# A gather on TensorE with its 128 output channels written as two instructions of 64 each

## The chip, the cores and the metric

The kernel runs on one core of one Trainium2 chip. The metric is the device time of one execution in microseconds (us). The kernel before took 786.88 us, the median of 3 runs (786.35 to 787.31). The profile shows one further execution; it took 786.77 us, of which the instructions' span covers 784.9 us.

## What is computed

All data is fp32. Layer 0 makes, for each pixel of 4 images of 256 channels and 64 x 64 pixels, 49 softmax weights and sums 49 shifted copies of the input with them. Layer 1 is a bottleneck block with batch statistics. Cut to what matters:

```python
# layer 0, x is (4, 256, 64, 64)
k = conv(x, w1, 7x7, dilation 2, padding 6) + b1      # 128 channels
attn = softmax(conv(k, w2, 1x1) + b2, axis=1)         # 49 weights per pixel
shifts = stack([xp[:, :, 2*u:2*u+64, 2*v:2*v+64] for u in range(7) for v in range(7)])
y = einsum('bkchw,bkhw->bchw', shifts, attn)
# layer 1
h = relu(bn(conv(y, w1, 1x1)))     # 256 -> 64 channels
h = relu(bn(conv(h, w2, 3x3)))     # 64 -> 64
return relu(bn(conv(h, w3, 1x1)) + y)   # 64 -> 256
```

## The kernel before

**Up to 490 us** the kernel computes the 49 weights per pixel: strided rows of the input are transformed on VectorE (the helper `stt`, L149), multiplied on TensorE (`column_convs`, L260), and turned into a matrix of weights by transposes (`turn`, L577). The weights end in `amat`, a part of the tile `arena`: for each image, column and parity the matrix that maps input rows to output rows.

**From 490 to 643 us** the gather runs together with layer 1's first conv; this is the part that the change touches. A unit is one image and one of four row and column parities; there are 16 units (L142). For each unit two tiles of input pixels by channels are needed: `x`, which three transfers load from HBM (`load_xt`: L111 and L117 small ones of 32 or 96 partitions, L112 the main one of 896 KB), and `t`, which is `x` shifted by 64 partitions (`shift_xt`: ScalarE copies one half, L121, GpSimd the other, L122 and L123). `more_xt` does this for unit n + 2 once unit n has been gathered, into the same tiles (two pairs alternate).

`gather(n, half)` makes 128 of the 256 channels of a unit. It takes two banks of PSUM, one for each column parity c, and issues 8 matmuls for each: seven for the tiles i = 1 to 7 with c = 0, the same for c = 1, and then the two edges (i = 0). The stationary operand is 128 pixels by 128 channels of `x` or `t`; the moving one is 128 columns of `amat`, in pieces of four elements. So a gather is 16 matmuls, and the stage has 32 gathers. The c = 0 matmuls read `x`, the c = 1 matmuls read `t`. Each fp32 matmul appears in the profile as two records of weight load and two of matmul, so that L765 has 1024 of each.

`keep_y` copies the two banks to a tile of SBUF, four copies for a gather: VectorE for half 0 (L786), ScalarE for half 1 (L784). Then SyncE's queue writes the tile to HBM (L787). `bank(0)` deals the gather's banks from five in turn.

`conv1` makes 64 channels from 256, for two units at once: 8 matmuls of 512 moving columns, whose outputs go to the partitions 0 to 63 (a = 0) or 64 to 127 (a = 1) of one bank. Two instructions that follow each other go to different halves. VectorE takes the statistics (L806) and copies a half (L812), ScalarE copies the other (L814).

The loop over units is: gather half 0; for an even n from 2 on `conv1` of the two units before; keep half 0; gather and keep half 1; load for n + 2. This part has no order written out by hand: a scheduler with its own estimates of cost orders each engine's instructions, and the DMA issues of SyncE. On TensorE it keeps the order of the loop, but for one place: the conv1 that belongs to unit 10 is broken up, and parts of unit 10's gather stand between its matmuls.

**From 643 us** the rest of layer 1 follows: direct and transformed 3x3 convs (L965, L977), transposes (L1040) and 64-channel products for the last batch statistics (`moments`, L1045, 65 moving columns, outputs to the two halves of the partitions in turn), and the last conv with the residual (L1027, L1084).

Of the kernel before, what the change touches and what calls it, by code (L numbers as in the profile page):

```python
# [48 lines left out]
P = 128  # L49
# [5 lines left out]
NT = H // 8  # L55
# [8 lines left out]
NP = len(PAIRS)  # L64
PIECES = ((0, 16), (16, 24), (40, 24))
READY = ((0, 1), (1, 4), (4, NT))
ROWS2 = 16
NS, WS = 4, 8
KV = K7 * K
# [24 lines left out]
def conv_seq_kernel(ctx: ExitStack, tc: tile.TileContext, xp, xt, w1, b1, w2t, b2, m1t, g1, be1,  # L94
                    m2t, g2, be2, m3t, g3, be3, z, mask, pavg, out, ydram):
    nc = tc.nc
# [41 lines left out]
    amat = arena[:, :AT].rearrange("p (g x c m e) -> p g x c m e", g=2, x=R // 2, c=2, e=4)  # L138
# [12 lines left out]
    def zero_rows(t):  # L151

        for k, i0, i1 in ((0, 0, 2), (1, 0, 1), (0, NR - 1, NR), (1, NR - 2, NR)):
            nc.gpsimd.memset(t[:, k, :, i0:i1], 0.0)
# [3 lines left out]
    def sort_x(raw, b, r0, n, dst, w0, last=None, first=None):  # L158

        d = dst.rearrange("p k (w b e) i -> p k w b e i", b=B, e=Q)  # L160
        nw = d.shape[2]
        for k in range(2):
            m = r0 // 2 + (r0 // 2 + 3 + k) % 2
            count = ((r0 + n) // 2 - m + 1) // 2
            i = (m + 3) // 2
            for a in range(2):
                lo = 2 * m + a - r0
                (last if last and k + a == 2 else first if first and k + a == 0 else nc.scalar.copy)(  # L168
                    d[:, k, :, PLACE[b], 2 * a : 2 * a + 2, i : i + count],
                    raw[:, lo : lo + 4 * count - 3 : 4, PAD + 2 * w0 : PAD + 2 * w0 + 2 * nw].rearrange(  # L170
                        "p r (w c) -> p w c r", c=2
                    ),
                )
# [41 lines left out]
    def rows_of(t, cols=slice(None), tiles=(0, NT)):  # L215


        def row(n):
            i = n // 2 + 2 * tiles[0]
            return t[:, n % 2, cols, i : i + 2 * (tiles[1] - tiles[0]) - 1 : 2]  # L220

        return row
# [50 lines left out]
    with ExitStack() as s1:  # L273
# [13 lines left out]
        with ExitStack() as s2:  # L287
# [71 lines left out]
            def early(n, cols=slice(None), parts=(even, odd, mix)):  # L359

                p, _, left = passes[0]
                t0, t1 = READY[n]
                x0, x1 = (xi[:, i, cols, t0:t1] for i in range(2))
                row = rows_of(slots, cols, READY[n])
                if even in parts:
# [78 lines left out]
        def fill_stage(h):  # L444
            zero_rows(stage)
            for r0 in range(0, H, ROWS2):
                for b in range(B):
                    raw = rawp.tile([P, ROWS2, WP], F32, tag="raw", name="raw")
                    nc.sync.dma_start(out=raw, in_=xp[b, P:, r0 : r0 + ROWS2, :])
                    sort_x(raw, b, r0, ROWS2, stage, R // 2 * h)  # L450

# [56 lines left out]
    for g in range(2):  # L508
        half = slice(g * MID, (g + 1) * MID)
# [165 lines left out]
    o = 4 * XT  # L675
# [3 lines left out]
    o = OUTER - NH1  # L679
# [33 lines left out]
    o = NH1  # L713
# [3 lines left out]
    o = 7 * C * 4  # L717
# [29 lines left out]
    def bank(kind):  # L747

        n_bank[kind] += 1
        return accall[:, 5 * kind + n_bank[kind] % (5 - 2 * kind)]  # L750

    def gather(n, half):

        b, q = units[n]
        m = (b // 2 * Q + q) * 2 * NT
        pts = [bank(0) for c in range(2)]
        for edge in (False, True):
            for c in range(2):
                x = xts[b, q, c]
                for i in (0,) if edge else range(1, NT):  # L760

                    o = 64 * (i - 1)
                    blocks = slice(m, m + 2 * NT, 2 * NT - 1) if edge else slice(m + 2 * i - 1, m + 2 * i + 1)
                    dst = pts[c].rearrange("p (m n) -> p m n", n=64)
                    nc.tensor.matmul(  # L765
                        dst[:, :: NT - 1] if edge else pts[c][:, o : o + 128],
                        x[:, i, half * P : (half + 1) * P],
                        amat[:, b % 2, :, c, blocks, :].rearrange("p x m e -> p m x e"),
                        start=(i == 1),
                        stop=edge,  # L770
                        skip_group_check=True,
                    )
        return pts

    def keep_y(n, half, pts):
# [41 lines left out]
    for n in range(len(units)):  # L817
        pts = gather(n, 0)
        if n and n % 2 == 0:
            conv1(*units[n - 2])  # L820
        if n == 9:
            clear_h1(1)
            nc.gpsimd.memset(w2blk, 0.0)
            for k, (j, a, o_a) in enumerate(TAPS3):
                d = TAP_ROW3[k]
                nc.sync.dma_start(
                    out=w2blk[a * MID : (a + 1) * MID, 3 * j : 3 * j + 3, o_a * MID : (o_a + 1) * MID],
                    in_=m2t[:, 3 * d : 3 * d + 3, :],
                )
        keep_y(n, 0, pts)  # L830
        keep_y(n, 1, gather(n, 1))
        if n + 2 < len(units):
            more_xt(n + 2)
# [175 lines left out]
    o = 4 * 2048  # L1009
# [24 lines left out]
    blocks = [(slot, i, q) for slot in range(2) for i in range(2) for q in range(Q)]  # L1034
    for n, (slot, i, q) in enumerate(blocks):
# [7 lines left out]
        for j in range(4):  # L1043
            for g in range(2):
# [4 lines left out]
                    start=(n == 0 and j == 0),  # L1049
                    stop=(n == len(blocks) - 1 and j == 3),  # L1050
                    skip_group_check=True,
# [14 lines left out]
    for half in range(NH):  # L1066
        c = slice(half * P, (half + 1) * P)
# [8 lines left out]
    blocks = [(slot + 2 * g, i, half) for slot in range(2) for i in range(2) for half in range(NH) for g in range(2)]  # L1076
    for k, (b, i, half) in enumerate(blocks):
        o = ops[k % 4]

        n = 256 if k in (0, len(blocks) - 1) else 512  # L1080
        for lo in range(0, 512, n):
            for q in (0, 2, 1, 3):
# [5 lines left out]
                dst = o[:, rows].rearrange("p (r a) (w c) -> p a c r w", a=2, c=2)[:, q // 2, q % 2]  # L1088
# [60 lines left out]
```

## Time and profile before

| what | value |
|---|---|
| median of 3 runs | 786.88 us |
| profiled execution | 786.77 us, span 784.9 us |
| TensorE matmul busy | 724.4 us, 92% of the span |
| VectorE, ScalarE, GpSimd busy | 74%, 39%, 11% |
| L260, column products | 2000 records, 384.4 us |
| L765, gather | 1024 records, 118.1 us, all between 490.4 and 638.8 us |
| L798, conv1 | 128 records, between 508.5 and 642.3 us |
| TensorE's granted clock in the stage from 488 to 645 us | 1.00 |
| DMA share in that stage | 0.65, 213 GB/s |

A line of a group names the line of the code, the engine, the operation, the tiles it writes and reads, the shapes, the number of records and their summed and mean time. A matmul's recorded duration includes its way through the array, and records overlap; how fast they follow each other is read from their starts. PEld is the weight load, which has its own records beside PE. `SPq` are the DMA issues of SyncE.

### The profile page before, as it was taken

To read this page: it belongs to the slowest core of one execution; us is meant where nothing else is said; L and a number is where in the kernel's file an instruction comes from. 1 tells how busy PE (TensorE), PEld (TensorE's weight loads), DVE (VectorE), ACT (ScalarE), POOL (GpSimd) and SP (SyncE) were. 2 spreads that over 40 slices of the span, in tenths; PEclk is the share of its full clock that TensorE was granted. 3 is DMA by queue.
4 is the path that set the end of the run, shared out by engine and by line. 5 is a ranking of instruction groups with operands and counts; after the bars stand their busy time and mean duration, and the time that the engine had idled before them with its cause. 6 is when DMAs were issued, how large, how long until landed. Compare 5 with 4: busy or idle time off the path is not lost.

```text
span 784.9 us, 10969 instructions
## 1 busy us (share of the span) xinstructions
PE 724.4 (92%) x4208; PEld 581.8 (74%) x4208; DVE 578.9 (74%) x685; ACT 305.2 (39%) x601; POOL 89.6 (11%) x155
## 2 busy tenths in 40 slices
PE   1969998999999989989999999999999979987996
PEld 1959887887888878878888888988877763436642
DVE  5799899999699689999998867233332247574796
ACT  4617465005621012111111158434443346346497
POOL 3416100001000010000003013222212200000000
PEclk9979998999999999999999999999999998997997
DMA  8741389626996985111110013666776659352298
GB/s 348 326 164 42 132 298 363 230 95 223 301 369 239 347 294 169 42 42 29 54 42 1 3 58 103 212 218 215 230 242 215 215 205 385 107 170 73 108 394 356
DMA packets 59814, 150.27 MB, mean 191 GB/s; under 512 B 7410, under 2 KB 35698, under 8 KB 56178
## 3 DMA queue, kind: packets, MB, share of 16 engines
q1 hardware_dynamic: 51792, 141.12, 50.4%
q10 hardware_dynamic: 7970, 8.45, 3.1%
q8 instruction: 33, 0.54, 0.3%
q14 instruction: 19, 0.16, 0.1%
HBM read 93.81 MB, written 55.74 MB: 191 GB/s over the span
## 4 chain that ended last, share of the span: by engine, by line
PE 58%; DVE 23%; DMA 8%; ACT 5%; issue 5%; ACTq 1%; POOL 0%; SPq 0%; DVEq 0%; POOLq 0%
PE acc L260 30%; DVE arena L149 13%; PE acc L765 12%; DVE arena L1084 4%; PE acc L798 4%; PE pconv L977 4%; PE pdirect L965 3%; DMA outer<-in_xt_dram 2%; DMA raw<-in_xp_dram 2%; PE acc L577 2%; DMA aside_dram<-sv 2%; DVE stage_x L149 1%; ACT arena L168 1%; PE pturn L1040 1%; ACT arena L584 1%
## 5 line engine op out<-in xcount | busy, mean ns | idle before, releaser
L260 PE MATMUL acc<-arena 128*128 128x196 f32 (+3 forms) x2000 | 384.4, 355 | 14.3 <-DVE arena L346 6.4
L260 PEld LDWEIGHTS acc<-arena 128*128 128x128 f32 x2000 | 323.8, 193 | 73.9 <-issue 13.1
L149 DVE SCALAR_TENSOR_TENSOR arena<-arena 128x1024 f32<-128x1024 f32 (+6 forms) x192 | 293.3, 1568 | 23.3 <-PE acc L260 17.0
L765 PEld LDWEIGHTS acc<-arena,outer 128*128 128x128 f32 x1024 | 115.5, 192 | 13.0 <-issue 10.9
L765 PE MATMUL acc<-arena,outer 128*128 128x128 f32 x1024 | 118.1, 276 | 4.9 <-issue 3.8
L806 DVE BATCH_NORM_STATS2 st<-acc 128x6 f32<-128x512 f32 x16 | 11.2, 699 | 68.3 <-PE acc L798 68.1
L284 ACT COPY sv<-acc 128x392 f32<-128x392 f32 x40 | 19.1, 484 | 92.3 <-PE acc L260 73.4
L168 ACT COPY stage<-raw 128x128 f32<-128x128 f32 x128 | 43.9, 417 | 23.6 <-DMA raw<-in_xp_dram 22.4
L1027 PE MATMUL pconv<-arena,w3m 64*128 64x512 f32 (+1 forms) x144 | 43.4, 597 | 0.6 <-DVE arena L1084 0.6
L121 ACT COPY outer<-outer 64x2048 f32<-64x2048 f32 x15 | 28.4, 1895 | 39.1 <-DMA outer<-in_xt_dram 39.0
L149 DVE SCALAR_TENSOR_TENSOR outer<-outer 128x784 f32<-128x784 f32 (+2 forms) x47 | 36.8, 835 | 3.6 <-ACT outer L919 3.6
L618 ACT COPY acc<-bks 128x392 f32<-128x392 f32 x40 | 18.3, 488 | 53.8 <-DVE outer L603 28.6
L601 ACT COPY outer<-acc 128x784 f32<-128x784 f32 x8 | 6.5, 813 | 79.7 <-PE acc L260 79.7
L1027 PEld LDWEIGHTS pconv<-arena,w3m 64*128 64x128 f32 x144 | 21.2, 189 | 21.6 <-DVE arena L1084 15.7
L786 DVE COPY bks<-acc 128x256 f32<-128x256 f32 x32 | 11.3, 416 | 33.4 <-PE acc L765 33.4
L122 POOL COPY outer<-outer 64x1792 f32<-64x1792 f32 x15 | 25.1, 1675 | 92.7 <-DMA outer<-in_xt_dram 92.6
L1089 ACT ACTIVATE outer<-arena 128x512 f32<-128x512 f32 (+1 forms) x58 | 34.7, 695 | 1.3 <-DVE arena L862 1.1
L1084 DVE SCALAR_TENSOR_TENSOR arena<-pconv,arena 128x512 f32<-128x512 f32 (+1 forms) x58 | 34.3, 666 | 0.0
L584 ACT COPY arena<-acc 128x512 f32<-128x512 f32 x52 | 27.1, 716 | 14.8 <-PE acc L577 14.4
L977 PE MATMUL pconv<-outer,arena 128*128 128x512 f32 x72 | 31.1, 592 | 0.0
L168 POOL COPY arena<-raw 128x192 f32<-128x192 f32 (+2 forms) x24 | 25.3, 1085 | 40.2 <-DVE arena L149 24.4
L798 PE MATMUL acc<-outer,w1m 128*64 128x512 f32 x64 | 29.6, 600 | 0.0
(147 smaller groups left out, 664.3 us busy)
## 6 DMA issues: line engine op xcount, KB each, us to landing
raw<-in_xp_dram SPq DMA_DIRECT2D x36, 608.0 KB, 5.4
outer<-in_xt_dram SPq DMA_DIRECT2D x17, 896.0 KB, 6.3
out_dram<-outer SPq DMA_DIRECT2D x14, 1024.0 KB, 4.5
arena<-y_dram SPq DMA_DIRECT2D x25, 512.0 KB, 8.0
fsort_dram<-stage SPq DMA_DIRECT2D x2, 4864.0 KB, 14.6
arena<-fsort_dram SPq DMA_DIRECT2D x8, 1216.0 KB, 9.3
y_dram<-outer SPq DMA_DIRECT2D x16, 512.0 KB, 5.4
aside_dram<-sv ACTq DMA_DIRECT2D x40, 196.0 KB, 5.5
```

Source lines behind the costliest of these rows:

```text
L121: nc.scalar.copy(t[:MID], x[MID:])
L122: nc.gpsimd.tensor_copy(t[MID:, : NT - 1], x[:MID, 1:])
L149: nc.vector.scalar_tensor_tensor(out, in0, scalar, in1, ALU.mult, ALU.add)
L168: (last if last and k + a == 2 else first if first and k + a == 0 else nc.scalar.copy)(d[:, k, :, PLACE[b], 2 * a : 2 * a + 2, i : i + count],
L260: nc.tensor.matmul(acc[i][d][:, o : o + (hi - lo) * K], xi[:, i, CW * w : CW * w + CW, :].rearrange("p x t -> p (x t)"), u[i][:, lo * K : ...
L584: nc.scalar.copy(dst, src)
L765: nc.tensor.matmul(dst[:, :: NT - 1] if edge else pts[c][:, o : o + 128], x[:, i, half * P : (half + 1) * P], amat[:, b % 2, :, c, blocks, ...
L798: nc.tensor.matmul(pt[a * MID : (a + 1) * MID, :], w1m[:, n, :], ys[a, n][:, 512 * i : 512 * i + 512], start=(n == 0), stop=(n == NH - 1), ...
L977: nc.tensor.matmul(m[k], wu[:, k, j, :], vs[k][:, g, j : j + R, :], start=(j == 0), stop=(j == 1))
L1027: nc.tensor.matmul(pt[:, :n], w3m[part, half * P : (half + 1) * P], h2[part, slot, q, lo : lo + n], start=True, stop=True)
L1084: nc.vector.scalar_tensor_tensor(v, conv3(b, q, i, half, lo, n), sc3[:, half : half + 1], v, ALU.mult, ALU.add)
L1089: nc.scalar.activation(dst, v.rearrange("p (r w) -> p r w", w=R), AF.Relu, bias=sh3[:, half : half + 1])
```

## The change

Each matmul of the gather becomes two. The first has the channels 0 to 63 of the half as its stationary operand and writes the partitions 0 to 63 of the bank, the second has the channels 64 to 127 and writes the partitions 64 to 127. Both have the same moving operand of 128 columns. The two stand next to each other in the program.

```diff
+HALVES = (slice(0, 64), slice(64, 128))
...
-                    nc.tensor.matmul(
-                        dst[:, :: NT - 1] if edge else pts[c][:, o : o + 128],
-                        x[:, i, half * P : (half + 1) * P],
-                        amat[:, b % 2, :, c, blocks, :].rearrange("p x m e -> p m x e"),
-                        start=(i == 1),
-                        stop=edge,
-                        skip_group_check=True,
-                    )
+                    for part in HALVES:
+                        nc.tensor.matmul(
+                            dst[part, :: NT - 1] if edge else pts[c][part, o : o + 128],
+                            x[:, i, half * P + part.start : half * P + part.stop],
+                            amat[:, b % 2, :, c, blocks, :].rearrange("p x m e -> p m x e"),
+                            start=(i == 1),
+                            stop=edge,
+                            skip_group_check=True,
+                        )
```

Nothing else of the program's text is changed; two lines are added, so that lines from 67 on stand one further down in the changed kernel, and lines from the matmul on two.

## Prediction, on record before the changed kernel ran

> **What bounds the kernel now.** I began with the page: TensorE is busy for 92% of the span, and the chain that ended last has 11.7% of the time on L765 and 3.7% on L798. Then I took the groups by line for the durations, the timeline of TensorE from 508 us on for the order, and the timelines of ScalarE and of SyncE's queue for what the stops in it wait on. From the page:
>
> ```profile
> PE 724.4 (92%) x4208; PEld 581.8 (74%) x4208; DVE 578.9 (74%) x685; ACT 305.2 (39%) x601; POOL 89.6 (11%) x155
> L765 PEld LDWEIGHTS acc<-arena,outer 128*128 128x128 f32 x1024 | 115.5, 192 | 13.0 <-issue 10.9
> L765 PE MATMUL acc<-arena,outer 128*128 128x128 f32 x1024 | 118.1, 276 | 4.9 <-issue 3.8
> ```
>
> In the gather the weight loads are busy as long as the matmuls. The timeline of TensorE shows their pace:
>
> ```profile
> 507.81 0.72 PE L765 MATMUL acc<-arena,outer 128*128 128x128 f32 x5
> 508.46 0.64 PE L798 MATMUL acc<-outer,w1m 128*64 128x512 f32 x1
> 508.47 0.64 PE L798 MATMUL acc<-bks,w1m 128*64 128x512 f32 x1
> 508.94 0.59 PE L798 MATMUL acc<-outer,w1m 128*64 128x512 f32 x1
> ...
> 511.52 0.59 PE L798 MATMUL acc<-outer,w1m 128*64 128x512 f32 x1
> ...
> 512.05 12.55 PE L765 MATMUL acc<-arena,outer 128*128 128x128 f32 x110
> 524.82 2.25 PE L765 MATMUL acc<-arena,outer 128*128 128x128 f32 x18 [0.22 <-issue]
> ```
>
> Three readings. First, the pace: 110 records take 12.55 us; less the last one's 0.275 us and one late step of 0.213, that is 108 steps of **111.7 ns**. The matmul alone does not need that: L260's of 147, 196 and 245 columns start 125, 166 and 206 ns apart, 0.83 ns a column, so 109 at 128, and L577's transposes of 128 columns do start 109 apart. Where L260 has 49 columns, its weight loads still follow each other 112 ns apart. So the gather goes at the pace of its 128-column weight load, with the matmul 2.5 ns behind. Second, conv1's two halves run together: both start at 508.46, and pairs follow every 0.43 us. Third, each change between the gather (128*128) and conv1 (128*64) costs time.
>
> The stop at 524.82 is a chain of its own:
>
> ```profile
> 515.74 1.20 ACT L784 COPY outer<-acc 128x256 f32<-128x256 f32 x4 [1.20 <-issue]
> 522.82 1.90 ACT L121 COPY outer<-outer 64x2048 f32<-64x2048 f32 x1 [5.88 <-DMA outer<-in_xt_dram]
> ```
>
> ```profile
> 513.94 0.38 SPq L112 DMA_DIRECT2D outer<-in_xt_dram  x1
> 514.41 2.89 SPq L787 DMA_DIRECT2D y_dram<-outer  x2
> 517.39 0.47 SPq L111 DMA_DIRECT2D outer<-in_xt_dram  x1
> 517.95 0.52 SPq L117 DMA_DIRECT2D outer<-in_xt_dram  x1
> ...
> 572.54 0.33 SPq L787 DMA_DIRECT2D y_dram<-outer  x1
> 572.92 0.43 SPq L112 DMA_DIRECT2D outer<-in_xt_dram  x1
> ```
>
> Unit 2's second gather ends at 515.6; L784 copies it out, L787 writes it, and behind it in SyncE's queue L111 and L117 load unit 4's edges. L121 shifts them until 524.7, and the c = 1 half of unit 4's gather starts: 9.1 us after 515.6. It then takes 18 records, conv1 and 32 records to the end of unit 4's second gather. So a round of two units lasts 9.1 + 50 steps + conv1, and the 78 steps beside it (unit 3 and half of 4) leave a gap. Units 4, 6, 8, 12 and 14 wait so (0.38, 0.41, 0.33, 1.99, 1.63 us over the step); rounds of 18.5 us, the last two 20.1 and 19.8.
>
> **The change part by part.**
>
> *Pace of the gather.* 1024 records of 128 output channels become 1024 pairs of 64. That adds 1024 weight loads and 1024 matmuls. The nearest rows are L798 and L1045, whose halves also alternate:
>
> ```profile
> 719.84 0.69 PE L1045 MATMUL moments<-outer 128*64 128x65 f32 x16
> 720.46 0.33 PE L1040 MATMUL pturn<-ident,arena 128*128 128x128 f32 x1
> 720.72 1.15 PE L1045 MATMUL moments<-outer 128*64 128x65 f32 x32
> 721.80 1.42 PE L1040 MATMUL pturn<-ident,arena 128*128 128x128 f32 x11
> 723.15 0.69 PE L1045 MATMUL moments<-outer 128*64 128x65 f32 x16
> ```
>
> Single records of L1045 at 729.935, 729.994, 730.052 and on show a pair every 58.5 ns, with two weight loads of 64 columns in it: the loads of the halves overlap too, so they hold no pair of 128 columns up. Between 58.5 ns at 65 columns and 429 at 512, a line gives **110.7 ns** at 128. Below, 109 (the matmul alone); above, twice 58.5, 117, if short pairs are limited by something that grows with their number; and twice 109, 218, if the halves cannot run together on this operand, which is a rival. I take 110.7, as both neighbours are pairs: 1.0 ns less a step.
>
> *Changes of shape.* Into conv1: last record of L765 at 508.255 (507.81 + 0.72 - 0.275), next start 508.46, 0.205 instead of 0.112; the first pair then holds 0.48 instead of 0.43. That is 0.144 us. Out of it: 511.52 to 512.05 instead of 0.43, and the next step 0.213 instead of 0.112: 0.20 us. All 10 entries and 9 exits from 508 to 639 us are like that, 3.2 us in all. With both in 128*64 they should go; the new one, from L577's transposes at 490.4, costs 0.1 more than now. The least that may go is nothing, if a change of 128 to 512 columns is what costs; L260's steps between widths show no such price, so I take all.
>
> [...]
>
> *Orders that move.* The scheduler gives new orders, read by comparing the programs. conv1 at unit 10 is whole: 8 entries and 7 exits are left. SyncE's queue now has L112 for unit 10 ahead of the second L787, so at about 569.5 instead of 572.92, when the first store has gone; elsewhere L787 of half 0 goes ahead of L112, ready about 0.1 us around it. L111 and L117 stay behind the second L787. VectorE's two L812 stand behind the four L786; nothing waits for them soon. ScalarE's L121 for odd units goes ahead of both L814, which then end at 515.2 (512.16 + 1.90 + two of 0.58), still before L784 at 515.74: hidden by 0.5 us, and each 0.1 us beyond it would go on the chain. GpSimd's order is unchanged. No wait is added; the copies out of PSUM wait for both halves of a bank, which end 7 ns apart.
>
> *The sum*, stretch by stretch:
> - 490.4 to 508.5: 160 steps at 1.0 ns, 0.16, less the dearer entry, 0.1: nothing.
> - Five rounds of the chain: 0.34 for the changes and 50 steps at 1.0 ns, 0.39 each: -1.95. The steps off the chain only widen the gap.
> - Unit 10: from 578.3 to the start of its second gather at 588.18 the trace has 9.9 us for 32 steps (3.54) and conv1 (3.43), so 2.9 us of waiting and three entries and exits. With L112 3 us earlier, L117 still issued near 573.4 and L121 ahead of L784, some 0.4 us of waiting stays: -2.5 (between -1.0, the changes alone, and -2.8).
> - From 624.5 on: one exit, two entries, 96 steps: -0.6.
>
> Together -5.05 us. From the profiled execution's 786.77 us that gives **781.7 us**; the median stands 0.11 us above it, which changes nothing. What follows at 643 us starts earlier by the same. At 109 ns it would be 781.1; at 117 (rounds of 128 x 0.117 + 3.48 = 18.46 us, no gap) 785.7. If the stores that go earlier in SyncE's queue also halved the five gaps (4.7 us), 779.3.
>
> **The rivals.**
>
> *The loads swallow it.* If the five rounds keep their length, because L117's landing (4.9 us here, 6.5 for unit 12) is set by the traffic and not by its issue, and unit 10 gains only its changes, 0.0 + 1.0 + 0.6 is left: 785.2 us. For it: two rounds are 1.5 us longer with the same work. Against: 213 GB/s in the stage, 453 at the most from 588 to 606.
>
> *Supply of instructions: slower.* A pair needs four instructions in 110.7 ns. L1040 and L1045 show 60 matmuls with their loads every 3.31 us (719.84 to 723.15), 55.2 ns a matmul, just what is needed (55.4), for some 10 us and with pauses. Over their whole stage, 710.6 to 731.63, it is 65.7 ns a matmul; that may be VectorE's pace, and may be the supply's. A round is then 128 pairs and 3.48 us with no gap left. Place: every stretch of L765. At 59.4 ns a matmul (118.8 a pair) the loss equals the gain; at 62.6, between the two rows, it adds 2.1 at the start, 1.0 in each of three rounds, 0.3 in two, 0.8 at the end, and unit 10 gains only 0.7: **792.6 us**.
>
> [...]
>
> *The halves do not run together.* The change would not do what it says: L798 and L1045 read runs of 64 bytes or more, the gather's moving operand pieces of 16 bytes, now twice at a time. One stream keeps up at 111.7. If they take turns, a pair costs 218 ns: 1024 x 0.1065 = 109 us less the changes and gaps, about 886 us.
>
> **How the numbers follow.** The forecast has 0.60, the swallowed gain 0.13, the supply 0.15, the turns (with all shares of them) 0.12. Two executions differ by 0.1%, so 0.2%, 1.6 us, can be told from no change. Faster: the forecast and half of the swallowed gain (785.2 lies on the edge), 0.67; same 0.06; slower 0.27. Range: from 777.5, two thirds of the gaps and unit 10's wait gone, to 793, which holds the supply and leaves out the turns.
>
> **What would show it.** Pairs of L767 (the new line) every 110 to 111 ns, weight loads no longer as busy as matmuls; first L800 after L767 at the normal step, and no 0.2 us step behind conv1; gaps before c = 1 still there, and at unit 10 under 0.5 us. A pace above 119, steps above 0.2 us around conv1, or rounds that stay at 18.5 us would prove me wrong.

## The result and the profile after

The changed kernel takes 783.38 us, the median of 22 runs (778.61 to 788.02), beside 786.90 us for the kernel before on the same chip (22 runs, 781.84 to 789.42). The ratio is 0.9964, with a 95% interval from 0.9947 to 0.9982: faster by 0.36%, where 0.66% had been forecast. The profiled execution took 784.71 us with a span of 782.9 us.

The lines of the page that answer to those of before; the gather is now L767:

```profile
PE 716.9 (92%) x5232; PEld 579.5 (74%) x5232; DVE 578.8 (74%) x685; ACT 304.7 (39%) x601; POOL 90.0 (12%) x155
L767 PEld LDWEIGHTS acc<-arena,outer 128*64 128x64 f32 x2048 | 112.7, 137 | 12.0 <-issue 11.4
L767 PE MATMUL acc<-arena,outer 128*64 128x128 f32 x2048 | 114.9, 273 | 6.7 <-issue 5.7
```

Twice as many records keep TensorE busy for 3.2 us less (114.9 for 118.1). The timeline of TensorE from conv1 of unit 2 on (L800 is conv1 now) shows how:

```profile
510.25 2.19 PE L767 MATMUL acc<-arena,outer 128*64 128x128 f32 x36 [0.45 <-issue]
512.23 0.59 PE L800 MATMUL acc<-outer,w1m 128*64 128x512 f32 x1
512.27 0.59 PE L800 MATMUL acc<-bks,w1m 128*64 128x512 f32 x1
...
515.27 0.59 PE L800 MATMUL acc<-arena,w1m 128*64 128x512 f32 x1
515.66 12.21 PE L767 MATMUL acc<-arena,outer 128*64 128x128 f32 x220
529.50 1.75 PE L767 MATMUL acc<-arena,outer 128*64 128x128 f32 x28 [1.62 <-issue]
```

The 220 records are 110 pairs. 12.21 us less the last record's 0.27 is 11.94 for 109 pairs and the offset of 0.04 between the halves. So a pair takes 109.2 ns where a whole product took 111.7. The first L800 record comes at once behind L767 (steps of 0.073 in place of 0.205 us), L767 follows conv1 after 0.39 us in place of 0.52, and its second step is normal. But the wait ahead of c = 1 in unit 4 is still there, and it is longer: 1.62 us idle where it was 0.22.

That wait is again the chain through ScalarE's copy (L786), the second store (L789), the edge loads (L112, L118) and the shift (L122). First ScalarE, then SyncE's queue, in the kernel after:

```profile
519.22 1.20 ACT L786 COPY outer<-acc 128x256 f32<-128x256 f32 x4 [0.81 <-ACT outer L816]
527.50 1.90 ACT L122 COPY outer<-outer 64x2048 f32<-64x2048 f32 x1 [7.08 <-DMA outer<-in_xt_dram]
```

```profile
517.11 0.34 SPq L789 DMA_DIRECT2D y_dram<-outer  x1
517.55 0.39 SPq L113 DMA_DIRECT2D outer<-in_xt_dram  x1
520.45 0.33 SPq L789 DMA_DIRECT2D y_dram<-outer  x1
520.87 0.38 SPq L112 DMA_DIRECT2D outer<-in_xt_dram  x1
521.34 1.01 SPq L118 DMA_DIRECT2D outer<-in_xt_dram  x1
```

Unit 2's second gather ends (start of its last pair) at 519.05. L118 is issued 2.29 us later; before it was 2.34. What has grown is the transfer: from L118's issue to the start of the shift it takes 6.16 us (521.34 to 527.50), where L117 took 4.87 (517.95 to 522.82). The interval from the end of one gather to the c = 1 half two units on, which the prediction kept at 9.1 us, came out like this (starts of single records, us):

| unit | 4 | 6 | 8 | 10 | 12 | 14 |
|---|---|---|---|---|---|---|
| before | 9.21 | 9.23 | 9.15 | 10.99 | 10.81 | 10.45 |
| after | 10.45 | 10.51 | 9.02 | 11.74 | 8.62 | 8.88 |
| after, second profile | 11.05 | 9.55 | 8.62 | 11.51 | 9.50 | 9.05 |

Without a wait it is 8.82 us for the whole products and 8.62 for the halves (e8 and e7 below). Steps of the gather over 0.24 us, other than the usual one behind conv1, add up to 6.8 us before and to 8.6 us after. From the first gather record to the start of the last conv1, called **the stage** from here on, the trace has 148.6 us before and 144.1 after: 4.5 us less, of which the whole execution kept 2.0, as it had started the stage 3.6 us later and ended 1.2 us sooner behind it. That start lies between 488.6 and 494.1 us in all the profiles of this study, in work that none of the kernels changes, so the stage tells more than a single total. It can be compared to a tenth of a microsecond only where nothing waits: the two profiles of the changed kernel have stages of 144.1 and 145.9 us, which differ by their waits.

### The profile page after: what moved, and what is told of

The parts are those of the page before. It is cut to its first block, busy times and chain, and to the rows that moved or that the text cites. A ratio compares the mean times of both kernels' runs of the same rounds, so it can differ in the third digit from the quotient of the medians.

```text
span 782.9 us, 13023 instructions
## 1 busy us (share of the span) xinstructions
PE 716.9 (92%) x5232; PEld 579.5 (74%) x5232; DVE 578.8 (74%) x685; ACT 304.7 (39%) x601; POOL 90.0 (12%) x155
## 4 chain that ended last, share of the span: by engine, by line
PE 59%; DVE 20%; DMA 9%; ACT 5%; issue 5%; POOL 1%; ACTq 1%; SPq 0%; DVEq 0%; POOLq 0%
PE acc L261 31%; DVE arena L150 13%; PE acc L767 9%; PE pconv L1029 4%; PE pconv L979 4%; DMA outer<-in_xt_dram 3%; PE acc L800 3%; PE pdirect L967 3%; DMA aside_dram<-sv 2%; PE acc L578 2%; DMA raw<-in_xp_dram 2%; DVE stage_x L150 2%; ACT arena L169 1%; PE pturn L1042 1%; ACT arena L585 1%
## 5 line engine op out<-in xcount | busy, mean ns | idle before, releaser
L261 PEld LDWEIGHTS acc<-arena 128*128 128x128 f32 x2000 | 324.9, 194 | 76.4 <-issue 13.1
L767 PEld LDWEIGHTS acc<-arena,outer 128*64 128x64 f32 x2048 | 112.7, 137 | 12.0 <-issue 11.4
L767 PE MATMUL acc<-arena,outer 128*64 128x128 f32 x2048 | 114.9, 273 | 6.7 <-issue 5.7
L808 DVE BATCH_NORM_STATS2 st<-acc 128x6 f32<-128x512 f32 x16 | 11.1, 695 | 66.3 <-PE acc L800 66.3
L122 ACT COPY outer<-outer 64x2048 f32<-64x2048 f32 x15 | 28.5, 1899 | 71.6 <-DMA outer<-in_xt_dram 71.6
L800 PE MATMUL acc<-outer,w1m 128*64 128x512 f32 x64 | 28.8, 592 | 0.0
```

Source lines behind the costliest of these rows:

```text
L122: nc.scalar.copy(t[:MID], x[MID:])
L261: nc.tensor.matmul(acc[i][d][:, o : o + (hi - lo) * K], xi[:, i, CW * w : CW * w + CW, :].rearrange("p x t -> p (x t)"), u[i][:, lo * K : ...
L767: nc.tensor.matmul(dst[part, :: NT - 1] if edge else pts[c][part, o : o + 128], x[:, i, half * P + part.start : half * P + part.stop], ama ...
L800: nc.tensor.matmul(pt[a * MID : (a + 1) * MID, :], w1m[:, n, :], ys[a, n][:, 512 * i : 512 * i + 512], start=(n == 0), stop=(n == NH - 1), ...
```

## The experiments

In the expectations the letters stand for one pair of theories in the first four runs and for others later; each text says for which. The prediction's chain is the theory behind all of them: the halves save TensorE's time, and the wait for the next tile gives it back. The rival: the halves themselves delay something. The runs were made on several chips, each beside the kernel before on the same chip, and each stage is that of one profile. All results in one table; "waits" are the gather's steps over 0.24 us, other than the usual one behind conv1, summed.

| kernel | ratio to before, 95% interval | stage, us | waits, us |
|---|---|---|---|
| before | 1 | 148.6 | 6.8 |
| after | 0.9964, 0.9947 to 0.9982 | 144.1 | 8.6 |
| e1 after, again | 0.9973, 0.9947 to 0.9999 | 145.9 | 8.7 |
| e2 halves, edges before second store | 0.9954, 0.9930 to 0.9979 | 147.1 | 10.0 |
| e3 whole, edges before second store | 0.9930, 0.9903 to 0.9957 | 143.7 | 2.9 |
| e4 halves, order of before | 0.9986, 0.9961 to 1.0010 | 148.8 | 11.7 |
| e5 halves, no loads | 0.9831, 0.9790 to 0.9872 | 135.9 | 0 |
| e6 whole, no loads | 0.9900, 0.9862 to 0.9937 | 141.0 | 0 |
| e7 halves, loads before stores | **0.9893, 0.9858 to 0.9928** | 135.9 | 0 |
| e8 whole, loads before stores | 0.9915, 0.9883 to 0.9946 | 141.0 | 0 |
| e9 halves in even units | 0.9883, 0.9828 to 0.9939 | 139.9 | 0 |
| e10 quarters | 1.0125, 1.0048 to 1.0203 | 153.5 | 13.1 |
| e11 halves not in turn | 1.0457, 1.0379 to 1.0535 | 185.1 | 0 |
| e12 whole, order of after | 0.9999, 0.9972 to 1.0027 | 149.3 | 2.2 |

**e1: the changed kernel once more.** No edit.

> The changed kernel once more, to see what of a single profile comes again. Both theories: pairs of the gather every 109 ns and steps of 0.07 and 0.39 us around conv1. Theory A (the new order of the DMA issues lengthens the rounds of units 4 and 6): these rounds last 19.0 to 19.6 us again, against 18.5 in the kernel before. Theory B (landing times of the loads differ from one execution to the next): they differ from 19.25 and 19.3 by over 0.5 us, and rounds of 17.4 to 20 us stand at other units than in the first profile. Time 782 to 785 us.

The wait ahead of c = 1 came back at unit 4 (2.5 us) and unit 10 (2.6), shrank at unit 6 (2.0 to 1.0) and vanished at unit 8. The landing of the edges moves by a microsecond from one execution to the next (unit 6's take 6.12 and 5.15 us, table under e12); that unit 10 waits over 2 us does not. The rounds of units 4 and 6 took 19.85 and 18.36 us where the first profile had 19.25 and 19.32, which is theory B.

**e2, e3 and e4: the order of SyncE's queue.** Here and in the runs behind, the issues of SyncE have an order written by hand, and each store is a call of its own (`store_y`), taken out of `keep_y`. For e2 (halves) and e3 (128 channels in one instruction):

```diff
+            store_y(n, 0)
+            pts = gather(n, 1)
+            load_xt(x, *units[n + 2], parts="mef")   # main, then the two edges
+            keep_y(n, 1, pts)
+            store_y(n, 1)
+            shift_xt(t, x)
```

In e4 (halves) the order is that of the kernel before in its regular rounds: for even n the main load, store, store, edges.

> The changed kernel with SyncE's order written out: the three loads of unit n + 2 go ahead of the store of unit n's second half, so they no longer wait for ScalarE's copies. Theory A (part of the gain went into gaps, because each round waits for the small loads behind that store): the gaps before c = 1 fall below 0.3 us but at unit 10, rounds last 17.4 to 17.8 us, the stage from the first gather to the last conv1 takes 136 to 139 us instead of 144.1, and the kernel is 5 to 8 us faster than the changed one, 776 to 779 us. Theory B (landing is set by the traffic): the loads land as late as before, the stage takes 143 to 145 us, and the time stays within 2 us of the changed kernel.

> The kernel before (128 channels in one matmul) with that same order of the loads. With e2, the kernel before and the changed one it makes a square of pace and shape against order. Theory A: rounds limited by TensorE, 128 x 0.1117 + 3.43 + 0.35 = 18.1 us, stage 141 to 143 us instead of 148.6, total 780 to 782 us, and e2 is 5 to 6 us faster still, the full price of weight loads (2.8) and changes of shape (3.0). Theory B: 786 to 788 us, and e2 less than 4 us faster.

> The changed kernel with the order of DMA issues that the kernel before has in its regular rounds (main load of an even unit ahead of both stores, small loads behind the second). Theory A (the order that the scheduler moved costs): the rounds of units 4 and 6 fall from 19.3 to 18.0 or 18.2 us, the stage to 142 to 143 us, total some 2 us below the changed kernel. Theory B (landing times vary by execution): no change that can be told, stage 143.5 to 145 us.

With the edges ahead of the second store the whole version lost most of its waits (6.8 to 2.9 us), much as theory A had it, but the halves had 10.0 us of them beside 8.6, with a time that cannot be told from that of the changed kernel. Theory A failed there. Where these waits come from stands in e2's timelines, of ScalarE, VectorE and SyncE's queue in turn:

```profile
510.23 1.91 ACT L125 COPY outer<-outer 64x2048 f32<-64x2048 f32 x1 [5.22 <-DMA outer<-in_xt_dram]
512.04 0.57 ACT L824 COPY outer<-acc 64x512 f32<-64x512 f32 x1
```

```profile
512.71 0.70 DVE L822 COPY outer<-acc 64x512 f32<-64x512 f32 x1 [2.21 <-ACT outer L824]
513.44 0.70 DVE L816 BATCH_NORM_STATS2 st<-acc 128x6 f32<-128x512 f32 x1
514.06 0.74 DVE L791 COPY outer<-acc 128x256 f32<-128x256 f32 x2
```

```profile
514.82 0.34 SPq L798 DMA_DIRECT2D y_dram<-outer  x1
515.27 0.38 SPq L116 DMA_DIRECT2D outer<-in_xt_dram  x1
```

The shift of the odd unit (L125) waits for its own load; conv1's copy (L824) stands behind it on ScalarE; VectorE's L822 waits for that one, and the last two copies of the gather (L791) stand behind L822; the first store (L798) needs them, and unit 4's main load L116 stands behind the store. One late landing so delays the next load by 2 us: L116 is issued 8.35 us after the start of the conv1 before it (506.92), L115 of e3 6.32 us after it (510.43). In e3 VectorE has three of the four L789 ahead of that wait. The order of the queue alone, as in e4, brought the halves nothing (11.7 us of waits), against theory A. So the width of the instruction and the waits cannot be told apart while loads wait behind stores.

**e5 and e6: no loads after unit 1.** Units 2 to 15 multiply the pixels of units 0 and 1, so that these kernels compute something else with the same products, copies and stores.

```diff
-            if n + 2 < len(units):
-                more_xt(n + 2)
+            if n + 2 < len(units):
+                xts[(*units[n + 2], 0)], xts[(*units[n + 2], 1)] = xtiles[2 * (n % 2) : 2 * (n % 2) + 2]
```

> Leaves out all input loads and shifts of units 2 to 15: their gathers read the tiles of units 0 and 1, so the products of these units are of the wrong pixels; every product, copy and store is still made. Theory A (the halves save their whole time on TensorE, and the changed kernel loses a part of it again only because c = 1 gathers wait for the next tile): no step above 0.24 us is left except perhaps at a bank or a store; rounds of two units are 17.4 us (128 pairs of 109 ns and 8 pairs of conv1 at 0.43), and the stage from the first gather record to the start of the last conv1 is 135 to 137 us, 4.5 to 6 us shorter than the same kernel with 128 channels in one instruction. Theory B (the halves themselves hold the stage up: banks, copies out of PSUM or stores come late at the higher pace): gaps above 0.24 us stay, over 2 us in all, and the difference is under 3 us.

> The same with 128 channels in one instruction, loads and shifts of units 2 to 15 left out too. Theory A: rounds of 18.05 to 18.1 us (128 steps of 111.7 ns, conv1 of 3.43 us and 0.34 for the two changes of shape), stage 140 to 142 us. Theory B: the same stage, as nothing but the loads' waits is taken away here.

Both came out as theory A has it: no wait is left, rounds of 17.41 us against 18.07, stages of 135.87 and 140.96 us. So **the halves are worth 5.09 us** where nothing waits, and no bank, copy or store holds TensorE up at their pace.

**e7 and e8: all loads ahead of both stores.**

```diff
+            keep_y(n, 0, pts)
+            pts = gather(n, 1)
+            load_xt(x, *units[n + 2], parts="mef")
+            store_y(n, 0)
+            keep_y(n, 1, pts)
+            store_y(n, 1)
+            shift_xt(t, x)
```

> All loads of unit n + 2 are issued ahead of both stores of unit n. Theory A: the tile for c = 1 lands earlier than with any other order, waits shrink to under 3 us in all, stage 136 to 140 us, and the kernel's time is 776 to 781 us. Theory B: the stage stays at 144 to 147 us since the stores now come later and hold up the tiles they read.

> The same order of the queue with 128 channels in one instruction. Theory A: waits under 2 us, stage 141 to 143 us, time 779 to 783 us, 2 to 5 us behind the halves with this order. Theory B: the same as the halves or faster.

The loads are all made again, and the stages are those of e5 and e6 to the hundredth: 135.87 and 140.96 us. SyncE's queue in e7, in which unit 2's second gather ends at 516.17:

```profile
514.56 0.38 SPq L116 DMA_DIRECT2D outer<-in_xt_dram  x1
516.27 0.33 SPq L114 DMA_DIRECT2D outer<-in_xt_dram  x1
516.69 0.37 SPq L121 DMA_DIRECT2D outer<-in_xt_dram  x1
517.16 0.85 SPq L798 DMA_DIRECT2D y_dram<-outer  x2
```

The last edge is issued 0.52 us behind the gather instead of 2.3, and in e7's ScalarE the shift begins 4.6 us later:

```profile
521.30 1.90 ACT L125 COPY outer<-outer 64x2048 f32<-64x2048 f32 x1 [3.78 <-DMA outer<-in_xt_dram]
```

It ends at 523.2, and c = 1 of unit 4 starts at 524.79: 1.6 us in hand. TensorE of e7, then of e8, from one conv1 (L808, L806) to the next:

```profile
512.78 14.14 PE L770 MATMUL acc<-arena,outer 128*64 128x128 f32 x256
526.76 0.59 PE L808 MATMUL acc<-outer,w1m 128*64 128x512 f32 x1
```

```profile
515.52 14.56 PE L768 MATMUL acc<-arena,outer 128*128 128x128 f32 x128
530.01 0.64 PE L806 MATMUL acc<-outer,w1m 128*64 128x512 f32 x1
```

From the first record behind conv1 to the next conv1 it is 13.98 us against 14.49. The 0.66 us of a round are 128 x 2.5 ns = 0.32 for the pace and 0.34 for the two changes of shape. By its stage e7 is the fastest of the kernels that compute everything. By the times alone e7 and e8 are not told apart (their intervals overlap); by the stage the halves are 5.1 us ahead.

**e9, e10 and e11** keep e7's order and alter only the slices of the product.

```diff
-                    for part in HALVES:
+                    for part in HALVES if n % 2 == 0 else (slice(0, P),):            # e9
...
-HALVES = (slice(0, 64), slice(64, 128))
+HALVES = tuple(slice(32 * i, 32 * i + 32) for i in range(4))                         # e10
...
-                for i in (0,) if edge else range(1, NT):
-                    for part in HALVES:
+                for part in HALVES:                                                  # e11
+                    for i in (0,) if edge else range(1, NT):
```

> All loads ahead of the stores, as in the version without waits, but only the even units in halves; the odd units take 128 channels in one instruction. So each round has 64 steps of each kind and two changes between 128*128 and 128*64 at the same 128 moving columns, and conv1 lies between two gathers in halves. If the change of the array's shape is what costs (theory A), a round is 64 x 0.1117 + 64 x 0.109 + 8 x 0.43 + about 0.34 for two changes = 17.9 us, the long steps stand at the borders of units and none at conv1. If only a change of the moving size costs (rival), 17.56 us plus steps of 0.2 us around conv1 and none at the borders of units.

Theory A: the rounds are 17.91 us. conv1 now lies between halves without a long step, and the borders of units, where the moving operand stays at 128 columns and only 128*128 turns to 128*64 or back, have the steps of 0.205 and 0.213 us. Here it is the shape on the array that costs, not the moving size: a change into the halves and one back cost some 0.34 us together.

> All loads ahead of the stores, and each product in four slices of 32 channels in four strips of the array's columns: 8 instructions of matmul and weight load for each step instead of 4. If four run together and the supply of instructions keeps up at 13.6 ns each: 109 ns for four, rounds of 17.4 us and up to 0.35 more, as conv1 then changes the shape again. If the supply ends near 27 ns an instruction (the halves run just at it), or only two of four run together: 218 ns for four, rounds of 31.4 to 31.7 us, and the kernel 110 to 115 us longer, about 890 us.

Neither: four slices do run together, at a median of 110 ns for four, 27.5 ns a matmul, but not for long. The timeline of e10:

```profile
515.20 12.34 PE L770 MATMUL acc<-arena,outer 128*32 128x128 f32 x412
...
543.40 7.25 PE L770 MATMUL acc<-arena,outer 128*32 128x128 f32 x246 [1.38 <-issue]
...
563.08 7.18 PE L770 MATMUL acc<-arena,outer 128*32 128x128 f32 x244 [1.82 <-issue]
```

14 stops of 0.28 to 2.1 us, 13.1 in all, fall in the middle of gathers, where no buffer begins. Counted in TensorE's instructions (two for a record of matmul), the stops from 543 us on are 254, 764, 256, 254, 766, 254, 764, 254 and 1020 apart, that is, one block of 254 to 256, three or four. The trace's DMA packets of kind instruction on queue q8 are 16,384 bytes each. They are TensorE's: from 490 to 640 us the kernel before has 9 of them and the changed one, with 2048 more instructions on TensorE, 17, which makes 256 instructions a packet; in the whole execution it is 33 of them for 8416 instructions and 41 for 10,464, 255 a packet. Each of the 14 stops ends 0.9 to 1.6 us after the end of such a packet. By these times TensorE runs to the end of a block before the next is there. In e7 a block lasts 7 us (256 at 27.3 ns) and none of these stops is seen; here it lasts 3.5 (256 at 13.8).

> All loads ahead of the stores, and the halves not in turn: seven products into the lower half, then the seven into the upper half. Theory A (a half is free while the other runs, and the pace comes from their overlap): followers wait for the one before on the same half, so each matmul takes 109 ns of its own, a step 218, rounds 31.3 us, the kernel 107 to 112 us longer, 880 to 890 us. Rival (two halves are no more than two short weight loads, each matmul starts as soon as its load is in): about the 109 ns of the alternating ones, and no more than 5 us longer.

In between: 23.6 us a round, or (23.6 - 3.4) / 128 = 157 ns a step, where 218 would have made 31.3 us. The timeline of e11 at the border of gather and conv1:

```profile
517.56 0.59 PE L807 MATMUL acc<-outer,w1m 128*64 128x512 f32 x1
517.61 0.49 PE L769 MATMUL acc<-arena,outer 128*64 128x128 f32 x3
517.94 0.59 PE L807 MATMUL acc<-bks,w1m 128*64 128x512 f32 x1
```

conv1's first product (lower half) starts while three records of the upper half, earlier in the program, have not. The same shows within the gather: of each run of 14 records in a half, the first few start beside the last four of the run before, and the rest stand alone at 109 ns; a period of 14 records takes 1.149 us, 82 ns a record, where halves in turn take 54.6. So TensorE takes work for the free half ahead of its turn, but in these starts only some four matmul records deep. Alternating is what makes the two halves cost as much as one product: 109.2 ns a step in turn, 157 here.

**e12: 128 channels in one instruction with the order of the changed kernel** (store, main, store, edges).

> 128 channels in one instruction, with the changed kernel's order of SyncE's queue in its regular rounds: first store, main load, second store, two edge loads. Theory A (the order of the loads sets the waits, whatever the width): from the end of a unit's second gather to the c = 1 half two units on takes 10 to 11 us in several rounds as in the changed kernel, waits of 6 us or more in all, stage 147 to 150 us, and the changed kernel's halves gain their 4 to 5 us on it. Rival (the halves themselves make the transfers land later): the chain keeps the 9.2 us it has in the kernel before for units 4, 6 and 8, waits under 3 us, stage 143 to 145 us, level with the halves or faster.

By its waits this does not answer its question: with the new order of the queue the scheduler also broke up conv1, in every round, as it had done at unit 10 in the kernel before. Unit 4's c = 1 half starts 10.1 us behind the gather's end, behind conv1's first piece, and nothing waits long, yet rounds are 19.26 us where e8 has 18.07. A broken conv1 so costs 1.2 us by itself, waits aside: two more changes of shape, and products that stand alone instead of in pairs (its first two records take 1.00 us, 526.73 to the gather's next at 527.73, where a pair takes 0.43).

The landings of the loads, which the trace has from the semaphores, answer more. From the issue of the second edge to its landing, us:

| kernel | unit 4 | unit 6 | unit 8 |
|---|---|---|---|
| before | 4.77 | 4.82 | 4.75 |
| e12, whole | 4.80 | 4.54 | 4.32 |
| after | 6.06* | 6.12* | 4.58 |
| after, second profile | 6.65* | 5.15* | 4.26 |
| e4, halves | 6.48* | 6.50* | 5.03 |

With whole products the edges land as early with the one order of the queue as with the other; with halves they land late in either, in units 4 and 6. Where a star stands, one of TensorE's packets of 16,384 bytes begins 3.4 to 4.8 us ahead of the landing; elsewhere none begins between 1.1 and 5.9 us ahead. The kernels with all loads together show the same. For units 4 to 8 of e7, e8, e9 and e11 the three loads take 5.2 to 5.7 us without such a packet up to their last microsecond, 6.3 to 6.9 us with one that begins 2.2 to 2.6 us ahead of the landing, and 5.8 to 6.6 us in the three cases with one earlier. So theory A is not borne out, and its rival has a likely carrier: the halves double the gather's instructions, and fetching them falls among the loads. That is a match in time; no run moves a fetch alone, so the cause is not shown, and at unit 14 the match fails (5.71 us before and 6.76 in e12 without a packet in that stretch, 4.53 in the changed kernel with one 2.1 us ahead).

## Why the prediction was right, and where its sizes were off

- *Pace of the gather*: right in kind, too small. I took 110.7 ns a pair from a line through two neighbours; it is 109.2, next to the lower bound of 109, which by L260's 0.83 ns a column is what the matmul alone needs. The saving is 2.5 ns a step, not 1.0; 128 of them make 0.32 us of a whole round.
- *Changes of shape*: right. All are gone; e9 shows the cause, and e7 against e8 gives 0.34 us a round, as was taken.
- *Start, "nothing"*: the first round grew from 18.02 to 18.16 us. The halves save 0.5 there (18.03 and 17.52 in e8 and e7), and c = 1 of unit 2 then waited 0.6 us. I had not asked there what is late next.
- *Five rounds of the chain at -0.39 each*: the five rounds changed by +0.72, +0.76, -0.65, -2.58 and -2.09 us, -3.8 in all where -1.95 was forecast (unit 12's is taken from the start of unit 10's second gather, where the prediction put the border). In units 4 and 6 the rounds grew to 19.25 and 19.32 us, which by the prediction's own signs speaks against it; the last two lost waits of 1.99 and 1.63 us that had stood in the one profile of before. The step that failed is **the chain of constant length**: I had put 9.1 us from one execution into every round. The length is set by a transfer that takes 4.9 us in one round and 6.2 or 6.8 in the next execution, and the halves, which come to the wait earlier, only turn what they save into idle time when it is long. That the edges land later in units 4 and 6 of both profiles of the changed kernel, with the same bytes ahead of them in the queue, goes with a fetch of instructions among these transfers (under e12). Why those of units 12 and 14 land earlier is not settled.
- *Unit 10 at -2.5*: the larger miss, -0.2 measured from the start of the conv1 before it to that of its second gather (24.16 to 23.98 us). The main load moved as forecast: L113 is issued 5.9 us after the start of the conv1 before it, where L112 came at 8.9 (572.92 against 564.02) and 5.5 had been expected. But the edges and the shift did not hold their places. ScalarE, then SyncE's queue of the kernel after, with that conv1 starting at 568.62 and unit 8's second gather ending at 575.44:

```profile
576.66 0.42 ACT L735 ACTIVATE arena<-arena 128x256 f32<-128x256 f32 x1 [2.03 <-DMA arena<-in_m2t_dram]
576.99 0.39 ACT L736 COPY arena<-arena 128x256 f32<-128x256 f32 x1
577.28 1.18 ACT L786 COPY outer<-acc 128x256 f32<-128x256 f32 x4
...
585.18 1.90 ACT L122 COPY outer<-outer 64x2048 f32<-64x2048 f32 x1 [5.49 <-DMA outer<-in_xt_dram]
```

```profile
574.53 1.10 SPq L113 DMA_DIRECT2D outer<-in_xt_dram  x1
578.49 0.33 SPq L789 DMA_DIRECT2D y_dram<-outer  x1
578.91 0.38 SPq L112 DMA_DIRECT2D outer<-in_xt_dram  x1
579.34 1.24 SPq L118 DMA_DIRECT2D outer<-in_xt_dram  x1
```

  Two instructions that prepare a later conv (L735, L736) stand ahead of the copy L786 on ScalarE and wait for their own load, so the copy starts 1.8 us behind the gather. The store waits for the copy and L118 for its turn behind the store: 10.7 us after conv1's start, where L117 came at 9.4. In the kernel before the same two started without a wait. The shift starts 5.8 us after L118's issue, 16.6 us after conv1's start in both kernels. But the late issue is not the whole of it. L113 landed 8.8 us after its issue (L112 7.5 before), the second store 1.2 us behind it, and the last edge 0.5 behind the store. In both kernels the last edge comes last in one line of transfers, behind a load of 512 KB for a later conv (L897; L895 before), two stores and the main load; the scheduler changed only the order within the line. In e7, where the loads stand ahead of both stores and of the loads for the later conv, the edges of unit 10 land 10.6 us after conv1's start. In the changed kernel TensorE, which is earlier, waits:

```profile
583.50 1.75 PE L767 MATMUL acc<-arena,outer 128*64 128x128 f32 x28 [0.76 <-DMA outer<-in_xt_dram]
587.18 2.19 PE L767 MATMUL acc<-arena,outer 128*64 128x128 f32 x36 [1.93 <-issue]
```

  The step that failed is "L117 still issued near 573.4 ... some 0.4 us of waiting stays": 3.0 us of it stayed (1.04 and 2.20 us of steps). What it left out: the main load moved up by 3.0 us in a busy queue, and the end of the queue did not come forward (the shift at 16.6 us in both). The second profile of this kernel shows the same, 2.8 us.
- *The end at -0.6*: -0.59.
- *The sum*: 0.14 - 3.84 - 0.18 - 0.59 = -4.47 us for the stage, where -5.05 was forecast. That it came so near is in part luck: unit 10 brought 2.3 us less than forecast and the five rounds 1.9 us more, by waits at units 12 and 14 that the forecast did not touch. The second profile of the changed kernel has a stage 2.7 us shorter than before. The medians differ by 3.5 us; the difference to the stage is within what the stage's start and its waits move from run to run.

The rivals. *The loads swallow it* was half true: of the 5.09 us that TensorE saves, the waits took some back, 8.6 us of them against 6.8. The measured 783.4 us lies midway between the forecast of 781.7 and this rival's 785.2, so the number alone does not choose between them; the traces show a part of both. *Supply of instructions* does not hold for the pace of the halves: 54.6 ns a matmul for 256 records in a row (e7), with no stop. These 54.6 ns, and e10's 27.5, lie below the 62.6 that this rival's sum took between two rows, so it is not the limit here. The supply shows only as e10's stops at the blocks and, as far as the times match, as fetches that delay loads. *The halves do not run together* is refuted for halves in turn; e11 shows how it would have come true.

## What to carry to other kernels

Two halves of the array's columns, written in turn, cost here what the matmul alone costs (109.2 ns a pair beside 109), and the change to conv1, which has that shape, cost nothing more (0.34 us a round less than for whole products); look ahead of it whether the weight load or the matmul sets the pace, count the instructions that it adds, and do not go as narrow as e10, where a block of 256 instructions lasted 3.5 us and TensorE stopped for 13.1 us in all. A saving on the busiest engine arrives in full only where nothing else is late: here it was 5.09 us of the stage without waits, 4.5 and 2.7 us in the two profiles with them, and a hand-written order with the loads ahead of the stores was worth 7.6 us of the stage to the old width and 8.2 to the new one, more than the change itself. And where a wait is to shrink because a load moves up, follow the last of the loads it needs, not the largest: all that the queue moves ahead of it, the store in front of it, the copy which that store waits for, and what stands ahead of the copy on its engine.

## What the runs showed of the hardware that was not expected

- Column halves in turn, 128 moving fp32 columns: 109.2 ns a pair, four instructions, without a stop for 13.9 us (e7). Quarters: four matmuls with their loads in 110 ns at the median (e10).
- TensorE started products of a free half ahead of up to about four earlier ones of the busy half (e11, conv1's first at 517.56 ahead of three from 517.61 on).
- At 3.5 us a block, TensorE stopped 14 times for 0.3 to 2.1 us at borders of 254 to 256 of its instructions (e10); at 7 us it did not (e7, no step over 0.24 us but the usual ones).
- An edge load of 96 KB took 4.3 to 6.8 us from issue to use, with the same work queued; in units 4 to 8 the long ones are those with a 16 KB packet of TensorE's instructions among the transfers ahead of it (a match in time).
